# Sums of features and column products of a gated mixture of experts: which engine adds, which engine carries

## Chip, core and metric

One Trainium2 chip, one core. The metric is the device time of one launch in microseconds (us). Engine names in the profile: PE is TensorE's matmuls and PEld its weight loads, DVE is VectorE, ACT is ScalarE, POOL is GpSimd, SP is SyncE, which issues most transfers.

## What is computed

For each of 8 sequences (512 rows of 256 features, float32) eight experts and one shared expert are computed, weighted and added to the input:

```python
def _L0_cond_ref(hidden_states, gating_probs, shared_gate_prob, Wg, Wu, Wd, Sg, Su, Sd):
    E, B, S, D, F = (8, 2, 256, 256, 1024)
    h = hidden_states
    g = jnp.einsum('bsd,edf->ebsf', h, Wg)
    u = jnp.einsum('bsd,edf->ebsf', h, Wu)
    expert_outs = jnp.einsum('ebsf,efd->ebsd', jax.nn.silu(g) * u, Wd)
    expert_output = jnp.einsum('be,ebsd->bsd', gating_probs, expert_outs)
    shared = jnp.einsum('bsf,fd->bsd', jax.nn.silu(h @ Sg) * (h @ Su), Sd)
    sg = shared_gate_prob[:, :, None]
    return (1.0 - sg) * expert_output + sg * shared
x = x + _L0_cond_ref(x, ...)
```

The first line's sizes are not used; the arrays have 8 sequences of 512 rows, weights of 256 x 1024 and 1024 x 256 and nine experts with the shared one.

## The kernel before

**Units.** The work is cut into 36 units: two halves of four sequences, nine experts, two groups of four blocks of 128 hidden features. A unit takes four sequences times four blocks, 16 pairs (i, j), and finds the gate and the up product of each pair with fewer matmuls than the plain way: sums and differences of weight blocks and of sequences are made first, and results are shared between pair (i, j) and pair (j, i). `PAIRS` lists the six such couples. A unit whose `opens` is set is the first of a half, one whose `closes` is set the last.

**Two generators.** `gate_up` yields 52 steps per unit, one matmul each: 16 hub steps (`P_step`, `Q_step` for the four pairs (i, i), and the first couple's `R1_step`), then six per couple (`R1_step`, `R_step`). `finish` applies silu on ScalarE (L391) and makes the weighted feature block h on VectorE (L396). `down` yields 26 steps per unit, one matmul each, on two PSUM banks po0 and po1 that take turns: three for each couple (r, s or S, and a third with X, the difference of two h), four row products p0 to p3 and four column products q0 to q3, in the order 0, 1, 2, 3, 4, p0, q0, 5, q1, p1, q2, p2, q3, p3.

**Order.** The string `ORDER` interleaves them, two G (a step of `gate_up`) to one D (a step of `down`). `down` of a unit begins at its 22nd G, so the row and column products of a unit run in the hub of the next unit and just behind it. The order on PE and POOL is that of the program (`HAND`); after the first unit the order on ACT and DVE is chosen by the scheduler that places the instructions.

**Feature sums.** A row product needs the sum over j of h[i, j], a column product the sum over i of h[i, j]. `h_sums` puts four entries per couple into the list `u.sums`, 24 per unit; the entries of couple (i, j) are rows i, cols j, rows j, cols i. `add_sum` (L480) takes the first of the list and makes one GpSimd addition of 128 x 512 (L486). The first addition to a sum adds the diagonal block h[n, n] and another, with a new tile from `sumpool`. The main loop calls `add_sum` on every second G after the 22nd, and in the next unit on every G until the list is empty; `flush_sums` makes what is still missing before a product needs it.

**Accumulation.** Results of `down` gather over the units of a half in SBUF tiles `acc`: B for columns, b for rows, V and S for parts of both. `put` adds a bank into such a tile on VectorE (L516 to L520), or copies on ScalarE when the tile is new. `carried` does it through the bank: `seeded` takes the next bank with `new_po`, ScalarE copies the tile into it (L528), the matmul accumulates on top (L529), and ScalarE copies the bank back (L537). If the tile is new, or the bank was last used for a transpose (`turned`), the matmul starts from zero and `put` follows. The rows use `carried`; the columns use `single` (a matmul that starts from zero) and `put`. A closing unit also uses the bank of a column product, `done`, to form the final tiles.

**Work beside it.** From the third unit on, every fifth D takes a step of `prepare(1)`, which transposes the second half's input and forms its sums (POOL lines L211 to L217).

Of the kernel before, what the change touches and what calls it, by code (L numbers as in the profile page):

```python
# [11 lines left out]
ALU = mybir.AluOpType  # L12
# [4 lines left out]
def kernel(  # L17
# [38 lines left out]
    B, S, D = x.shape  # L56
# [38 lines left out]
    gp = nc.gpsimd  # L95
    ve = nc.vector
# [35 lines left out]
    def new_po(name, turns=False):  # L132

        k = po_next[0]
        if held[k]:
            k = 1 - k
        if not turns:
            po_next[0] = 1 - k
        return ps_o.tile([P, S], F32, tag=f"po{k}", name=name), k
# [144 lines left out]
    for h in range(NH):  # L284
        for e in range(NE):
            for g in range(GRP):
                u = Unit()
                u.n, u.h, u.e, u.g = len(units), h, e, g
                u.opens = e == 0 and g == 0
                u.closes = e == NE - 1 and g == GRP - 1  # L290
                u.name = f"{h}_{e}_{g}"
                u.raw, u.at, u.U, u.W, u.V, u.VB = {}, {}, {}, {}, {}, {}
                u.Ps, u.Ds, u.f, u.bank, u.h_ = {}, {}, {}, {}, {}
                u.sg, u.rows, u.cols, u.X, u.store = {}, {}, {}, {}, []
                u.sums = []
                u.ad, u.Ud, u.Wd = {}, {}, {}
                units.append(u)

# [181 lines left out]
    def add_sum(u):  # L480
        which, n, at = u.sums.pop(0)
        sums = getattr(u, which)
        first = n not in sums
        if first:
            sums[n] = sumpool.tile([P, S], F32, tag="sum", name=f"{which}{n}_{u.name}")
        gp.tensor_tensor(sums[n], u.h_[n, n] if first else sums[n], u.h_[at], ALU.add)  # L486

    def flush_sums(u, which, n):
        while any(w == which and k == n for w, k, _ in u.sums):
            add_sum(u)  # L490
# [5 lines left out]
    def closes(u, p):  # L496

        return u.closes and starred(u, p) or u.n + 2 == len(units) and p >= 4

    def down(u, acc):  # L500

        def tile_of(key):
            acc[key] = apool.tile(
                [P, S], F32, tag=f"acc{key[0]}{key[1]}", name=f"acc{key[0]}{key[1]}_{u.h}"
            )
            return acc[key]

        def put(key, bank, s):

            if key not in acc:  # L510
                if s == 1.0:
                    nc.scalar.copy(tile_of(key), bank)
                else:
                    nc.scalar.mul(tile_of(key), bank, s)
            elif s == 1.0:
                ve.tensor_add(acc[key], bank, acc[key])  # L516
            elif s == -1.0:
                ve.tensor_sub(acc[key], acc[key], bank)
            else:
                ve.scalar_tensor_tensor(acc[key], bank, s, acc[key], ALU.mult, ALU.add)  # L520

        def seeded(key, w, b):

            po, k = new_po(f"{key[0]}{key[1]}_{u.name}")
            full = key in acc and not turned[k]
            turned[k] = False
            if full:
                nc.scalar.copy(po, acc[key])  # L528
            nc.tensor.matmul(  # L529
                po, w, b, start=not full, stop=True, skip_group_check=full  # L530
            )
            return po, full

        def carried(key, w, b):
            po, full = seeded(key, w, b)
            if full:
                nc.scalar.copy(acc[key], po)  # L537
            else:
                put(key, po, 1.0)
            return po if full else acc[key]  # L540

        def single(key, w, b):
            po, k = new_po(f"{key[0]}{key[1]}_{u.name}")
            turned[k] = False
            nc.tensor.matmul(po, w, b, start=True, stop=True)  # L545
            return po, k

        def pair(p):
            i, j = PAIRS[p]
            d = CI[i] - CI[j]  # L550
            A, k = single(("r", p), u.Wd[p][i], u.h_[i, j])
            put(("B", j), A, 1.0)
            held[k] = True
            yield
            args = u.Wd[p][j], u.h_[j, i]
            if p in OWN and not closes(u, p):
                carried(("S", p), *args)
            else:
                if p in OWN:
                    o, full = seeded(("S", p), *args)  # L560
                    if not full:
                        ve.tensor_add(o, o, acc["S", p])
                else:
                    o, _ = single(("s", p), *args)
                put(("B", i), o, -1.0)
                put(("V", p), o, -1.0)
            yield
            nc.tensor.matmul(  # L568
                A, u.Ud[p], u.X[p], start=False, stop=True, skip_group_check=True
            )  # L570
            if closes(u, p):
                ve.tensor_add(A, A, acc["V", p])
                put(("b", i), A, 1.0 / d)
                put(("b", j), A, -1.0 / d)
            else:
                put(("V", p), A, 1.0)
            held[k] = False
            po_next[0] = 1 - k
            yield

        if u.n + 1 < len(units):
            order = (0, 1, 2, 3, 4, "p0", "q0", 5, "q1", "p1", "q2", "p2", "q3", "p3")
        else:
            order = (0, 1, 2, "q0", 3, "p0", "q3", "q1", "p3", "q2", "p1", "p2")
        done = {}
        for what in order:
            if isinstance(what, int):
                yield from pair(what)
                continue
            i = int(what[1])  # L590
            if what[0] == "p":
                flush_sums(u, "rows", i)
                done[what] = carried(("b", i), u.raw_d[:, i, 0:P], u.rows[i])
            else:
                flush_sums(u, "cols", i)
                po, _ = single(("q", i), u.ad[i], u.cols[i])
                put(("B", i), po, 1.0)
                done[what] = po
            if u.closes and f"p{i}" in done and f"q{i}" in done:
                if CI[i] != 0.0:  # L600
                    put(("B", i), done[f"p{i}"], -CI[i])
                for r in (0, 1):
                    ends[u.h, i, r] = acc["bB"[r], i]
            yield
# [183 lines left out]
    for u in units:  # L788
# [6 lines left out]
        for what in FIRST if u.n == 0 else LAST if nxt is None else ORDER:  # L795
            if what == "G":
                if nG == TAKE:
                    for _ in behind:
                        pass
                    if u.opens:  # L800
                        acc = {}
                    behind = down(u, acc)
# [7 lines left out]
                if nG > TAKE and nG % 2 == 0 or nxt is None:  # L810
                    for _ in range(2 if nxt is None else 1):
                        if u.sums:
                            add_sum(u)
                if nG < TAKE and u.n and units[u.n - 1].sums:
                    add_sum(units[u.n - 1])
# [7 lines left out]
            elif what == "X":  # L823
                i, j, pools = TAILS.pop(0)
# [59 lines left out]
```

## Time and profile before

Three runs gave 2463.46 us as a median (2463.18 to 2464.2).

| | us |
|---|---|
| profiled execution, its own time | 2464.21 |
| its span, first to last instruction | 2462.3 |
| PE busy in the span | 2439.2 |
| POOL busy | 2100.1 |
| DVE busy | 1936.5 |
| ACT busy | 1246.9 |
| mean granted TensorE clock | 0.999 of full speed |

The groups of instructions that the change touches, from the profile's table (line, engine, operation, output and inputs, shape, count; then busy us, mean ns of one, and idle time of the engine just before them):

```profile
L486 POOL TENSOR_TENSOR rows<-rows,h 128x512 f32<-128x512 f32 x284 | 373.9, 1316 | 0.0
L486 POOL TENSOR_TENSOR cols<-cols,h 128x512 f32<-128x512 f32 x284 | 363.3, 1279 | 0.0
L486 POOL TENSOR_TENSOR cols<-h,h 128x512 f32<-128x512 f32 x144 | 184.3, 1280 | 0.0
L516 DVE TENSOR_TENSOR accB<-q,accB 128x512 f32<-128x512 f32 x144 | 99.1, 688 | 41.7 <-PE q L545 41.3
L528 ACT COPY b<-accb 128x512 f32<-128x512 f32 x134 | 79.7, 595 | 52.6 <-DVE accV L518 39.2 <-DVE accB L516 5.1 <-DVE accb L520 3.4
L537 ACT COPY accb<-b 128x512 f32<-128x512 f32 x134 | 79.1, 590 | 36.5 <-PE b L529 33.7
L545 PE MATMUL q<-cols,ad 128*128 128x512 f32 x216 | 110.8, 595 | 4.8 <-POOL cols L486 3.3 <-DVE accB L520 1.4
```

One matmul of the program is two PE instructions in the trace, which overlap; a unit's length is read from the starts.

### The profile page before, as it was taken

The numbers are of one execution on the slowest core, as the hardware profiler recorded it, in microseconds if no ns is written. First come the engines' busy times: TensorE is split into PE (matmuls) and PEld (weight loads), VectorE is DVE, ScalarE is ACT, GpSimd is POOL, SyncE is SP. The second block draws the span as 40 slices with busy tenths as digits, with TensorE's granted clock in tenths as the row PEclk, the third lists the DMA queues.
The fourth block names the chain that finished last, engine by engine and source line by source line (L and its number), as shares of the span: only waits on it lengthen the run. The fifth ranks groups of instructions, "written<-read, shape, count | busy, mean of one in ns | idle before, by whom it ended". The sixth has DMA issues, their size and how long they took to land.

```text
span 2462.3 us, 22810 instructions
## 1 busy us (share of the span) xinstructions
PE 2439.2 (99%) x5772; PEld 1082.2 (44%) x5772; DVE 1936.5 (79%) x2880; ACT 1246.9 (51%) x2305; POOL 2100.1 (85%) x2339
## 2 busy tenths in 40 slices
PE   9999999999999999999999999999999999999998
PEld 3444444444444444444444444444444444444444
DVE  7777787787777777777987777777777777777788
ACT  4555445545555555445455555555555455555552
POOL 7988888898898998888878888888888888888884
PEclk9999999999999999999999999999999999999999
DMA  4333333443333333333443223323333333232332
GB/s 166 96 94 102 97 113 107 124 133 107 109 115 96 117 100 104 108 116 118 122 150 91 88 89 96 90 82 98 99 103 103 99 98 93 84 96 88 94 97 75
DMA packets 180800, 255.81 MB, mean 104 GB/s; under 512 B 14016, under 2 KB 114368, under 8 KB 180672
## 3 DMA queue, kind: packets, MB, share of 16 engines
q1 hardware_dynamic: 180384, 254.33, 33.9%
q8 instruction: 48, 0.79, 0.1%
q14 instruction: 80, 0.66, 0.1%
q10 hardware_dynamic: 288, 0.04, 0.0%
HBM read 238.59 MB, written 15.73 MB: 103 GB/s over the span
## 4 chain that ended last, share of the span: by engine, by line
PE 89%; POOL 6%; DVE 2%; issue 1%; DMA 1%; ACT 0%; SPq 0%; ACTq 0%; DVEq 0%; POOLq 0%
PE c L459 28%; PE c L449 14%; PE c L427 9%; PE c L405 8%; PE r L545 7%; PE r L568 7%; PE S L529 5%; PE b L529 5%; PE q L545 5%; PE s L545 2%; POOL cols L486 1%; POOL rows L486 1%; POOL wd L376 1%; DVE h L396 1%; POOL wb L343 0%
## 5 line engine op out<-in xcount | busy, mean ns | idle before, releaser
L459 PE MATMUL c<-b,wb 128*128 128x512 f32 x1728 | 847.2, 592 | 0.0
L391 ACT ACTIVATE sg<-c 128x512 f32<-128x512 f32 x576 | 343.9, 597 | 591.0 <-DVE c L464 336.1
L396 DVE SCALAR_TENSOR_TENSOR h<-sg,coef,c 128x512 f32<-128x512 f32 x576 | 428.1, 743 | 249.0 <-PE c L459 139.7
L459 PEld LDWEIGHTS c<-b,wb 128*128 128x128 f32 x1728 | 327.9, 190 | 411.0 <-issue 389.4
L449 PE MATMUL c<-v,u 128*128 128x512 f32 x864 | 441.7, 593 | 0.7 <-ACT c L444 0.7
L486 POOL TENSOR_TENSOR rows<-rows,h 128x512 f32<-128x512 f32 x284 | 373.9, 1316 | 0.0
L486 POOL TENSOR_TENSOR cols<-cols,h 128x512 f32<-128x512 f32 x284 | 363.3, 1279 | 0.0
L454 DVE TENSOR_TENSOR c<-D,c 128x512 f32<-128x512 f32 x432 | 299.0, 692 | 78.3 <-ACT sg L391 58.5
L464 DVE TENSOR_TENSOR c<-c,D 128x512 f32<-128x512 f32 x432 | 298.7, 691 | 20.2 <-PE c L459 20.0
L343 POOL TENSOR_TENSOR wb<-u,wb 128x256 f32<-128x256 f32 x108 | 78.8, 729 | 235.7 <-ACT wb L341 235.7
L405 PE MATMUL c<-x,w 128*128 128x512 f32 x576 | 278.1, 595 | 0.3 <-DVE x L166 0.3
L449 PEld LDWEIGHTS c<-v,u 128*128 128x128 f32 x864 | 162.9, 190 | 206.0 <-issue 165.6
L545 PE MATMUL r<-h,wd 128*128 128x512 f32 x428 | 218.8, 593 | 1.8 <-DVE accb L520 1.6
L568 PE MATMUL r<-X,ud 128*128 128x512 f32 x428 | 218.5, 592 | 0.0
L475 DVE TENSOR_TENSOR X<-h,h 128x512 f32<-128x512 f32 x214 | 211.6, 989 | 6.9
L427 PE MATMUL c<-x,at 128*128 128x512 f32 x432 | 209.6, 593 | 2.8 <-DVE P L420 2.7
L437 ACT COPY D<-c 128x512 f32<-128x512 f32 x284 | 166.0, 584 | 86.9 <-DVE h L396 86.9
L486 POOL TENSOR_TENSOR rows<-h,h 128x512 f32<-128x512 f32 x144 | 198.4, 1378 | 0.0
L486 POOL TENSOR_TENSOR cols<-h,h 128x512 f32<-128x512 f32 x144 | 184.3, 1280 | 0.0
L410 ACT COPY P<-c 128x512 f32<-128x512 f32 x216 | 126.7, 586 | 109.2 <-PE c L405 104.9
L405 PEld LDWEIGHTS c<-x,w 128*128 128x128 f32 x576 | 109.3, 191 | 135.1 <-issue 112.2
L528 ACT COPY S<-accS 128x512 f32<-128x512 f32 x135 | 79.7, 590 | 152.4 <-DVE accV L516 142.5
(106 smaller groups left out, 3480.8 us busy)
## 6 DMA issues: line engine op xcount, KB each, us to landing
b<-xs SPq DMA_DIRECT2D x210, 512.0 KB, 3.6
v<-xs SPq DMA_DIRECT2D x210, 256.0 KB, 2.6
w<-in_L_cond_Wg_dram SPq DMA_DIRECT2D x128, 128.0 KB, 3.5
w<-in_L_cond_Wu_dram SPq DMA_DIRECT2D x128, 128.0 KB, 3.6
wd<-in_L_cond_Wd_dram SPq DMA_DIRECT2D x32, 512.0 KB, 4.9
xin<-in_x_dram SPq DMA_DIRECT2D x24, 256.0 KB, 3.5
f<-xd SPq DMA_DIRECT2D x24, 256.0 KB, 3.2
xs<-f SPq DMA_DIRECT2D x18, 256.0 KB, 2.0
```

What stands on the lines that cost most here:

```text
L391: nc.scalar.activation(s, bank, AF.Silu)
L396: ve.scalar_tensor_tensor(t, u.sg[i, j], coef[:, u.e, b : b + 1], bank, ALU.mult, ALU.mult)
L405: nc.tensor.matmul(bank, u.raw[i][:, m, 0], xhub[u.h, i][:, 0], start=True, stop=True)
L427: nc.tensor.matmul(bank, u.at[i][:, m], xhub[u.h, i][:, 1], start=False, stop=True, skip_group_check=True,)
L449: nc.tensor.matmul(bank, u.U[p][:, m], u.V[p], start=False, stop=True, skip_group_check=True)
L454: ve.tensor_sub(other, u.Ds[j, m], bank)
L459: nc.tensor.matmul(bank, u.W[p][:, r, m], u.VB[p][:, r], start=False, stop=True, skip_group_check=True,)
L464: ve.tensor_add(bank, bank, u.Ds[j, m])
L486: gp.tensor_tensor(sums[n], u.h_[n, n] if first else sums[n], u.h_[at], ALU.add)
L529: nc.tensor.matmul(po, w, b, start=not full, stop=True, skip_group_check=full)
L545: nc.tensor.matmul(po, w, b, start=True, stop=True)
L568: nc.tensor.matmul(A, u.Ud[p], u.X[p], start=False, stop=True, skip_group_check=True)
```

## The change

Two edits. First, each unit counts its sums in `u.added`; the additions with number 3, 11 and 19 of the 24 (counted from 0) go to VectorE in units that neither open nor close a half. Second, the column products of all units but the two that close a half use `carried` with the key B, that is ScalarE's copy into the bank, an accumulating matmul and ScalarE's copy back, in place of a matmul from zero and VectorE's addition.

```diff
-                u.sums = []
+                u.sums, u.added = [], 0
...
-        gp.tensor_tensor(sums[n], u.h_[n, n] if first else sums[n], u.h_[at], ALU.add)
+        eng = ve if u.added % 8 == 3 and not (u.opens or u.closes) else gp
+        eng.tensor_tensor(sums[n], u.h_[n, n] if first else sums[n], u.h_[at], ALU.add)
+        u.added += 1
...
             else:
                 flush_sums(u, "cols", i)
+                if not u.closes:
+                    carried(("B", i), u.ad[i], u.cols[i])
+                    yield
+                    continue
                 po, _ = single(("q", i), u.ad[i], u.cols[i])
                 put(("B", i), po, 1.0)
                 done[what] = po
```

## The prediction

> **What bounds the kernel now.** I read four views, in this order: the busy shares, TensorE's own waits, TensorE's sequence unit by unit, and then the other engines beside it in one steady unit.
>
> ```profile
> span 2462.3 us, 22810 instructions
> PE 2439.2 (99%) x5772; PEld 1082.2 (44%) x5772; DVE 1936.5 (79%) x2880; ACT 1246.9 (51%) x2305; POOL 2100.1 (85%) x2339
> ```
>
> TensorE is busy for 99%, but a busy share does not say that matmuls run back to back, so the starts are needed. In the sequence of TensorE a single matmul is two instructions, and consecutive ones start 0.86 us apart (1453.07, 1453.93, 1454.79, ...). The same place in two neighbouring units, the two products (four instructions) that start at 1429.90 and at 1496.85, lies 66.95 us apart: 78 matmuls of 0.858 us, nothing over. Most of the 36 units are like this. TensorE is at its floor there, and no edit of other engines can shorten them; it can only lengthen them.
>
> What lies above the floor I got by taking, from each start to the next, the count of matmuls times 0.429 us per instruction (128-column transposes a quarter, 256-column products half). The work is 2423.4 us and the excess 33.5: 11.2 up to the end of the first unit, 8.6 in the last 95 us, and between them some 9 us of waits (the rest is missing records). What ended the waits between is in TensorE's list (total, times, longest):
>
> ```profile
> PE q L545 <- POOL cols L486: 3.3, 4, 1.2
> PE c L427 <- DVE P L420: 2.7, 3, 1.8
> PE S L529 <- ACT S L528: 1.7, 3, 0.6
> ```
>
> The first line is the one this change can touch: a column product waits for its sum on GpSimd. By start spacing those four cost 0.82 (at 96.43), 0.67 (638.98), 1.12 (841.06) and 1.35 us (1043.36). This is the costliest, first on TensorE and then on GpSimd:
>
> ```profile
> 1041.15 1.02 PE L427 MATMUL c<-x,at 128*128 128x512 f32 x2
> 1043.36 1.12 PE L545 MATMUL q<-cols,ad 128*128 128x512 f32 x2 [1.19 <-POOL cols L486]
> ...
> 1038.36 1.27 POOL L486 TENSOR_TENSOR cols<-cols,h 128x512 f32<-128x512 f32 x1
> 1039.58 1.28 POOL L486 TENSOR_TENSOR rows<-rows,h 128x512 f32<-128x512 f32 x1
> ...
> 1042.04 1.26 POOL L486 TENSOR_TENSOR cols<-cols,h 128x512 f32<-128x512 f32 x1
> ```
>
> The sum at 1042.04 feeds the product at 1043.36; GpSimd has no idle from 1008 to here, because this unit also carries steps of the second half's preparation (f, L211 to L217). The wait at 96.43 belongs to the sums of the first unit, which the change leaves on GpSimd.
>
> **The change part by part.** Own time of the profiled execution is 2464.21 us, 1.9 above its span and 0.75 above the median of 2463.46. The sum is made against 2464.21.
>
> (1) Three of 24 sums leave GpSimd in 32 units (36 less two that open and two that close a half): 96 x 1.28 us = 123 us off GpSimd. Counting calls, sums 3 and 11 fall in the unit itself (its 30th and 46th step), sum 19 in the next unit's hub (the 16 steps that mix x products of one's own block). In the view above sum 19 is the one at 1038.36, and the sum that q waits for is number 21 in the same queue. Without 19, number 21 starts 1.22 us earlier (1039.58 - 1038.36). Number 11 left the same unbroken queue 20 us before, worth up to another 1.2 us. That covers 0.67 and 1.12, and 1.35 with a little of number 11. Gain at most 0.67 + 1.12 + 1.35 = 3.1 us; at least 0, if GpSimd loses the time again. I take 2.8, nearest the upper end, since two of three are covered by sum 19 alone.
>
> (2) The three sums on VectorE. No such sum runs there now; the nearest is X, also two SBUF inputs and one SBUF output of the same size:
>
> ```profile
> L475 DVE TENSOR_TENSOR X<-h,h x214: 682/1056/1673, 38.1 to 2425.1; 128x512 f32<-128x512 f32 x107
> ```
>
> So 0.68 to 1.67, I take 1.06: 96 x 1.06 = 102 us more for VectorE. Where X runs beside GpSimd, one of the two is stretched: X is 0.69 at 1434.05, and the GpSimd addition that starts at 1434.11 takes 1.23 in place of 0.73; GpSimd's sums reach 1.73 in place of 1.27 (1493.81, with X at 1493.61). So a moved sum gives GpSimd 1.27 and takes up to 0.5 back. The Trainium skill, page "SBUF — State Buffer", section "Who interferes with whom", speaks against this edit: a VectorE instruction with two SBUF inputs holds a read port shared with GpSimd, and whichever starts second blocks until the other is done. The stretch of 0.5 agrees with it in kind; by the rule read strictly, a GpSimd sum would wait the whole 0.68 of an undisturbed sum, and the net gift would be 0.6 us a sum instead of 0.8.
>
> Cover for sums 3 and 11: VectorE waits 1.3 us in these blocks (before 1474.80 and 1490.25, both for a h buffer that GpSimd's rows still hold), and the next bank it must empty has slack: accV ends at 1477.47, the copy of S at 1478.1, its matmul starts 2.4 us later at 1480.54. Cover for sum 19: VectorE's idle 1.44 before 1436.84, and 0.57 plus the vanished addition of q0 (0.69) before 1439.44. Without cover a sum costs up to its 1.06 us of TensorE. I take 0.
>
> (3) The column product through its bank. There are four per unit in 34 units; rows already do this (134 copies in, 134 out), so about 134 again. VectorE loses 134 additions of 0.69 = 92 us; ScalarE gets 268 copies of 0.59 = 158 us. Over the span nothing is saturated: ScalarE goes from 1247 to 1405 us, VectorE from 1937 to 1946, GpSimd falls to 1977. But all column products fall into the hub and the block after it, so that stage decides:
>
> ```profile
> 1432.60:1453.20 20.60, 20.60 (x50) 9.12 (x49) 17.36 (x28) 11.99 (x22) 20.05 (x26) 1.00 0.11 31
> ```
>
> (TensorE, weight loads, VectorE, ScalarE, GpSimd, in 20.6 us.) ScalarE has 12.0 there and gets up to six copies, 3.5: 15.5 of 20.6, it fits. VectorE loses two additions (1.4) and gets sum 19 (0.7 to 1.2). A queue of its own does not run out; what can hurt is order. Each product's bank is needed two slots after it was used, 5.15 us. Before the product it must be emptied and filled:
>
> ```profile
> 1443.69 0.68 DVE L518 TENSOR_TENSOR accV<-accV,s 128x512 f32<-128x512 f32 x1
> 1444.79 0.75 DVE L396 SCALAR_TENSOR_TENSOR h<-sg,coef,c 128x512 f32<-128x512 f32 x1 [0.41 <-POOL rows L486]
> 1445.55 0.69 DVE L516 TENSOR_TENSOR accV<-r,accV 128x512 f32<-128x512 f32 x1
> 1446.41 3.68 DVE L420 TENSOR_TENSOR P<-P,c 128x512 f32<-128x512 f32 x6 [0.17 <-PE c L405]
> ...
> 1443.83 0.60 ACT L391 ACTIVATE sg<-c 128x512 f32<-128x512 f32 x1
> 1444.33 0.58 ACT L437 COPY D<-c 128x512 f32<-128x512 f32 x1
> 1445.57 0.59 ACT L437 COPY D<-c 128x512 f32<-128x512 f32 x1 [0.67 <-DVE h L396]
> 1446.27 0.59 ACT L528 COPY b<-accb 128x512 f32<-128x512 f32 x1
> ```
>
> q1 runs at 1447.06 in the bank that accV leaves at 1444.37. The new copy fits into ScalarE's idle 0.67 before 1445.57 and ends near 1445.5: slack 1.5 us. q0 (1436.76) follows accV at 1432.67 to 1433.36 with 2.8 us of slack for one copy. q1's copy out meets 2.98 idle before 1449.84; q2's out and q3's in meet 0.88 + 0.49 + 0.26 + 0.39 idle between 1452.4 and 1457.4, against 1.2. So I take 0 for TensorE. What is queued behind such a copy is the silu and D copies, and behind them h, the six f's at 1446.41 and the product at 1448.78: three f's, 0.60 apart, end at 1448.29, leaving 0.5 us. That is the thinnest cover in the unit. If a copy stands ahead of the silu at 1443.83, it ends at 1444.96, the silu at 1445.6, h starts 0.8 late, 0.17 of that is absorbed, and the f's are some 0.6 late: TensorE loses 0.1, and with the 0.16 that a restart adds (1.35 against 1.19 above) about 0.3. Bounds for (3): 0 to 0.3 a unit; were sum 19 also put just before the f's, 0.8 + 1.06 - 0.17 - 0.5 + 0.16 = 1.35, which I count with the second rival. A gain is excluded in steady units, which have no wait to give.
>
> **Sum.** 2464.21 - 2.8 + 0 + 0 = 2461.4 own time; 0.75 lower as a median, 2460.7 us.
>
> **The rivals.** About 0.2%, 4.9 us, is what can be told from no change.
>
> Hub late (slower): the copy into a column's bank stands in ScalarE's order ahead of the silu, as worked out. For it: ScalarE's and VectorE's order are not written by hand there, and the copies of S already stand waiting for accV, 142.5 us in 94 times, 1.5 each. Against: the same copies for rows cost TensorE nothing in steady units. 34 x 0.3 = 10.2: 2470.9; it decides from 0.5 us of lateness of the f's on. Chance 0.30.
>
> VectorE late (slower): a moved sum in the wrong place, as sum 3 or 11 before accV, delays S. In the closing unit three extra VectorE instructions (r and two on accb) do that, 0.72 us each time; one sum of 1.06 is less than their 1.9. If it happened once per unit, 32 x 0.72 = 23: 2484 (with 1.35 as above, 2504). Chance 0.08.
>
> No effect: GpSimd gains nothing where it matters, since sum 23 on GpSimd now waits for 19 on VectorE, or the stretch eats the gift: 2463.5. Chance 0.12.
>
> Faster beyond 0.2%: all 3.1 and both waits for accS ahead of transposes (1.12 and 0.97, at 194 and 339), 5.2: 2458.3. Nothing in the change leads to the second part. Chance 0.07.
>
> **How the numbers follow.** The forecast has 0.43, its own range 2459.5 to 2463. Of the hub rival's 0.30, 0.07 lies below 2468.4. Within 0.2%: 0.43 + 0.12 + 0.07 = 0.62; slower 0.23 + 0.08 = 0.31; faster 0.07. The range 2458.2 to 2473 leaves out that rival's 0.08, some 0.05 of the hub's end and 0.03 below.
>
> **What would show it.** Right: units still 66.95 us apart; no wait of a column product for GpSimd after the second unit; GpSimd near 1977 us, ScalarE near 1405. Hub late: waits of the matmuls behind L420, or of q for the copy in, in most units. VectorE late: waits of S for ScalarE in ordinary units. The prediction is wrong if units are longer than 67.1 us in steady stretches.

## The result, and the profile after

| | before | after |
|---|---|---|
| median, us (22 runs each, side by side) | 2463.21 | 2467.58 |
| profiled execution, its own time | 2464.21 | 2467.75 |
| its span | 2462.3 | 2465.8 |

The ratio is 1.0016, 95% interval 1.0010 to 1.0022: 4.4 us slower, where 2.8 us faster was forecast. (One run of each, 8235 us of after and 2857 of before, stands apart from all others and is used in no reading.) The time lies in the range of 2458.2 to 2473.0; its direction does not agree with the forecast. The busy shares of the kernel after:

```profile
PE 2443.7 (99%) x5772; PEld 1080.0 (44%) x5772; DVE 1967.8 (80%) x2842; ACT 1377.1 (56%) x2573; POOL 2020.1 (82%) x2243
```

Work moved as described: GpSimd has lost 96 instructions and 80 us, ScalarE has gained 268 copies. None of the engines beside TensorE has become full. The groups that the change made (busy us and mean ns of one, then idle time just before them):

```profile
L487 DVE TENSOR_TENSOR cols<-h,h 128x512 f32<-128x512 f32 x64 | 86.8, 1355 | 0.0
L530 ACT COPY B<-accB 128x512 f32<-128x512 f32 x134 | 80.4, 600 | 41.6 <-DVE accV L518 40.5
L539 ACT COPY accB<-B 128x512 f32<-128x512 f32 x134 | 78.4, 585 | 41.1 <-PE B L531 41.1
L487 DVE TENSOR_TENSOR cols<-cols,h 128x512 f32<-128x512 f32 x32 | 39.8, 1242 | 0.0
```

A sum on VectorE takes 1.24 to 1.36 us on average, not the 1.06 assumed. TensorE's own waits in the kernel after (total us, times, longest):

```profile
PE ptx L143 <- ACT accS L539: 2.9, 2, 1.9
...
PE B L531 <- POOL cols L487: 0.6, 1, 0.6
```

Against the list of before: column products wait for GpSimd once instead of four times (the one left stands at 95 us, in the opening unit's sums), so the three waits of 3.1 us in all are gone. The transposes of the second half's input wait longer (2.9 instead of 1.8). Nothing in the list is as large as the loss, because the largest part of it is too short for this list. It shows in the starts: the unit that the prediction measured, from 1429.90 to 1496.85, is now the pair at 1430.99 and 1498.07, 67.08 us apart instead of 66.95. The 0.13 more stand at one place in each unit. TensorE's sequence there:

```profile
1476.48 1.02 PE L570 MATMUL r<-X,ud 128*128 128x512 f32 x2
1477.39 1.10 PE L449 MATMUL c<-v,u 128*128 128x512 f32 x2
1478.33 1.02 PE L459 MATMUL c<-b,wb 128*128 128x512 f32 x2
```

The matmul at 1477.39 was due at 1476.48 + 0.86 = 1477.34, 0.05 late; the next one follows after 0.94 instead of 0.86, 0.08 more. So 0.13 a unit, and 32 x 0.13 = 4.2 us. What it waits for is on VectorE and ScalarE (the number in brackets is idle time before the instruction and what ended it):

```profile
1470.76 0.74 DVE L396 SCALAR_TENSOR_TENSOR h<-sg,coef,c 128x512 f32<-128x512 f32 x1
1471.41 1.35 DVE L487 TENSOR_TENSOR cols<-h,h 128x512 f32<-128x512 f32 x1
1472.68 1.21 DVE L475 TENSOR_TENSOR X<-h,h 128x512 f32<-128x512 f32 x1
1473.81 0.68 DVE L454 TENSOR_TENSOR c<-D,c 128x512 f32<-128x512 f32 x1
1474.41 0.68 DVE L518 TENSOR_TENSOR accB<-r,accB 128x512 f32<-128x512 f32 x1
1475.01 0.68 DVE L464 TENSOR_TENSOR c<-c,D 128x512 f32<-128x512 f32 x1
...
1475.73 0.60 ACT L391 ACTIVATE sg<-c 128x512 f32<-128x512 f32 x1 [3.11 <-DVE c L464]
1476.22 0.58 ACT L539 COPY accS<-S 128x512 f32<-128x512 f32 x1
1476.69 0.61 ACT L444 COPY c<-P 128x512 f32<-128x512 f32 x1
```

The same instructions of before:

```profile
1470.43 1.23 DVE L475 TENSOR_TENSOR X<-h,h 128x512 f32<-128x512 f32 x1
...
1472.79 0.68 DVE L464 TENSOR_TENSOR c<-c,D 128x512 f32<-128x512 f32 x1
...
1473.50 0.60 ACT L391 ACTIVATE sg<-c 128x512 f32<-128x512 f32 x1 [1.98 <-DVE c L464]
1474.13 0.59 ACT L444 COPY c<-P 128x512 f32<-128x512 f32 x1
1474.66 0.58 ACT L537 COPY accS<-S 128x512 f32<-128x512 f32 x1
...
1476.25 1.02 PE L449 MATMUL c<-v,u 128*128 128x512 f32 x2
```

The reader is to see a chain that crosses three engines: sum 3 stands ahead of X on VectorE, so X, L454, accB and L464 come later; ScalarE's silu waits for L464 (3.11 instead of 1.98); behind the silu stand the copy of S and the copy that seeds the next couple's bank (L444), and TensorE's L449 accumulates onto that bank. Measured against TensorE, the seed ended at 1474.72, 1.53 before its matmul; now it ends at 1477.30, 0.04 before the matmul was due. The matmul starts 0.09 after that end by these rows, hence 0.05 late; in all 31 units where the trace has both records, the distance is 0.10 by the unrounded times. The 1.49 lost are the sum, 1.27 from its start to X's, less about 0.14, and about 0.35 for the copy of S, which ScalarE now makes between the silu and the seed.

The sum of the traces' differences: 4.2 (32 units), 0.5 (a wait of 0.47 at 2377 us in the last unit for a carried column's copy in), -3.1 (the column products' waits), 1.1 (the wait at 339 us), 1.7 (TensorE's clock just behind it), 0.6 (once at 531 us), -1.1 (the start) = 3.9. The spans differ by 3.5; some matmul records are missing, which the difference of 0.4 may be.

### The profile page after: what moved, and what is told of

Same layout as the page of the kernel before. It is cut to its first block, busy times and chain, and to the rows that moved or that the text cites. A ratio compares the mean times of both kernels' runs of the same rounds, so it can differ in the third digit from the quotient of the medians.

```text
span 2465.8 us, 23011 instructions
## 1 busy us (share of the span) xinstructions
PE 2443.7 (99%) x5772; PEld 1080.0 (44%) x5772; DVE 1967.8 (80%) x2842; ACT 1377.1 (56%) x2573; POOL 2020.1 (82%) x2243
## 4 chain that ended last, share of the span: by engine, by line
PE 94%; DVE 3%; POOL 1%; issue 1%; ACT 0%; DMA 0%; SPq 0%; DVEq 0%; ACTq 0%; POOLq 0%
PE c L459 29%; PE c L449 14%; PE c L427 9%; PE c L405 9%; PE r L547 7%; PE r L570 7%; PE S L531 5%; PE b L531 5%; PE B L531 5%; PE s L547 2%; DVE h L396 1%; POOL cols L487 0%; PE tail L657 0%; POOL rows L487 0%; DVE X L475 0%
## 5 line engine op out<-in xcount | busy, mean ns | idle before, releaser
L459 PE MATMUL c<-b,wb 128*128 128x512 f32 x1728 | 848.3, 593 | 0.0
L459 PEld LDWEIGHTS c<-b,wb 128*128 128x128 f32 x1728 | 328.1, 190 | 411.1 <-issue 392.5
L449 PE MATMUL c<-v,u 128*128 128x512 f32 x864 | 444.1, 595 | 2.0 <-ACT c L444 1.5
L454 DVE TENSOR_TENSOR c<-D,c 128x512 f32<-128x512 f32 x432 | 299.2, 693 | 136.6 <-ACT sg L391 94.0
L487 POOL TENSOR_TENSOR cols<-cols,h 128x512 f32<-128x512 f32 x252 | 335.8, 1333 | 0.0
L343 POOL TENSOR_TENSOR wb<-u,wb 128x256 f32<-128x256 f32 x108 | 78.7, 729 | 278.9 <-ACT wb L341 278.9
L464 DVE TENSOR_TENSOR c<-c,D 128x512 f32<-128x512 f32 x432 | 298.2, 690 | 5.5 <-PE c L459 2.9
L449 PEld LDWEIGHTS c<-v,u 128*128 128x128 f32 x864 | 160.3, 189 | 214.2 <-issue 163.6
L475 DVE TENSOR_TENSOR X<-h,h 128x512 f32<-128x512 f32 x214 | 222.3, 1039 | 4.7
L570 PE MATMUL r<-X,ud 128*128 128x512 f32 x428 | 219.1, 594 | 0.0
L343 POOL TENSOR_TENSOR wb<-u,w 128x256 f32<-128x256 f32 x108 | 89.0, 824 | 94.9 <-PE c L459 91.7
L531 PE MATMUL S<-h,wd 128*128 128x512 f32 x288 | 147.9, 595 | 1.8 <-ACT S L530 1.7
```

What stands on the lines that cost most here:

```text
L449: nc.tensor.matmul(bank, u.U[p][:, m], u.V[p], start=False, stop=True, skip_group_check=True)
L454: ve.tensor_sub(other, u.Ds[j, m], bank)
L459: nc.tensor.matmul(bank, u.W[p][:, r, m], u.VB[p][:, r], start=False, stop=True, skip_group_check=True,)
L464: ve.tensor_add(bank, bank, u.Ds[j, m])
L487: eng.tensor_tensor(sums[n], u.h_[n, n] if first else sums[n], u.h_[at], ALU.add)
L531: nc.tensor.matmul(po, w, b, start=not full, stop=True, skip_group_check=full)
```

## The experiments

All edits are made to the changed kernel. Where only the condition of the moved sums differs, the diff gives that line. Each was timed beside the kernel before, whose median was between 2463.0 and 2463.2 us in all of them. The theory: a sum that stands ahead of L464 on VectorE uses up the 1.53 us that the seed copy had. The rival: the carried columns' copies, on ScalarE, make something late.

**The two halves of the change.** Columns carried alone (cols_only):

```diff
-        eng = ve if u.added % 8 == 3 and not (u.opens or u.closes) else gp
+        eng = ve if False else gp
```

> The column products are carried through their bank, no sum is moved. Theory (a sum on VectorE in the third block of a unit delays the seed copy ahead of a matmul of L449 by 0.13 us in each of 32 units): units are 66.95 us apart again, the three waits of column products for GpSimd (0.7 to 1.4 us each) are back, 2463 to 2464 us. Rival (ScalarE's copies of the columns in the hub cost the time): units stay at 67.08 us, 2467 us or more.

Sums moved alone (sums_only):

```diff
-                if not u.closes:
-                    carried(("B", i), u.ad[i], u.cols[i])
-                    yield
-                    continue
```

> Sums 3, 11 and 19 on VectorE, the column products as in the kernel before. Theory: units 67.08 us apart or longer with the small waits at L449 in the third block, no wait of a column product for GpSimd after the second unit, 2466 to 2468 us. Rival (the columns' copies): units 66.95 us apart, 2460 to 2461 us.

Measured: cols_only 2464.2 us, ratio 1.0005 (0.9995 to 1.0014); sums_only 2466.87, ratio 1.0015 (1.0006 to 1.0024). In cols_only units are 66.95 us apart and the three waits for GpSimd are back. TensorE's waits there:

```profile
PE B L531 <- POOL cols L487: 3.4, 4, 1.2
```

This is the old line of q under a new name: same four times, same longest. In sums_only the units have the 0.13, and none of these three waits is there. So the lengthening of the units belongs to the sums, and the rival falls: the carrying of columns leaves the units as they were and is close to neutral in the median.

**Which of the three sums.** cols_s19, cols_s11_19 and cols_s3 carry the columns and move only these sums:

```diff
+        eng = ve if u.added == 19 and not (u.opens or u.closes) else gp
...
+        eng = ve if u.added in (11, 19) and not (u.opens or u.closes) else gp
...
+        eng = ve if u.added == 3 and not (u.opens or u.closes) else gp
```

> Columns carried, of the three sums only number 19 on VectorE. Theory: units 66.95 us apart, the waits of column products for GpSimd in the units at 639, 841 and 1043 us gone or under 0.3 us each, no drop of the granted clock at 339 us: 2460 to 2461 us. Rival (columns' copies): 2467 us. Rival (GpSimd needs all three to be relieved): the three waits stay, 2463 us.

> Columns carried, sums 11 and 19 on VectorE, 3 back on GpSimd. Theory: units 66.95 us apart; the transposes at 339 us still wait about 2 us, since sum 11 stands in the block before them, and the clock drops behind them in some runs: 2461 to 2463 us. If sum 11 is as harmful per unit as sum 3, units are 67.08 us apart and the time is 2466 us.

> Columns carried, of the three sums only number 3 on VectorE. Theory (sum 3 alone is the cost): units 67.08 us apart, with the small wait at L449 in the third block of each; the three waits of column products for GpSimd partly back; 2466 to 2468 us. If the loss needs sums 3 and 11 together, units are 66.95 us apart and the time is 2463 us.

| | median us | ratio (95%) | unit | waits of column products for GpSimd behind the start |
|---|---|---|---|---|
| cols_s19 | 2461.47 | 0.9993 (0.9984 to 1.0003) | 66.95 | none at 639, 0.34, 0.60 |
| cols_s11_19 | 2461.41 | 0.9994 (0.9985 to 1.0004) | 66.95 | none |
| cols_s3 | 2468.78 | 1.0026 (1.0015 to 1.0036) | 67.08 | 0.68, 1.13, 1.37 |

One sum out of three carries the whole lengthening of the units. The time of cols_s3 is 0.8 above the range expected: besides 32 times 0.13 its trace has 0.59 at 528 us, in place of one of the 0.05, and the 0.47 in the last unit, 5.2 in all against 5.6 by the medians. cols_s19 keeps more of the waits than expected (under 0.3 each) and is 0.5 above its range. Sums 11 and 19 together give what the prediction said of all three: no waits and unlengthened units. Sum 3 gives all the harm and none of the relief, which had been expected in part. The relief is lost at a line that stands between it and the column products. GpSimd at 1007 us in cols_s3 (in the kernel before, the same instruction stands at 1006.78 with 2.04 of idle time ahead of it):

```profile
1007.80 0.73 POOL L343 TENSOR_TENSOR wb<-u,wb 128x256 f32<-128x256 f32 x1 [2.18 <-ACT wb L341]
```

GpSimd idles here for ScalarE's wb whether sum 3 was its own or not. The time of sum 3 was gone even before this: GpSimd's addition beside it, at 995.95, takes 1.72 instead of 1.26, and ahead of L343 at 999.36 GpSimd idles for 1.70 instead of 0.92, where it waits for TensorE. Time given to GpSimd ahead of an idle stretch only lengthens the idle stretch; sums 11 and 19 are behind it, in the stretch without idle that ends in the wait.

**More of the suspected cost.** cols_s3x2 is cols_s3 (with its condition) and makes sum 3's addition twice, with the same result:

```diff
-        eng.tensor_tensor(sums[n], u.h_[n, n] if first else sums[n], u.h_[at], ALU.add)
+        for _ in range(2 if eng is ve else 1):
+            eng.tensor_tensor(sums[n], u.h_[n, n] if first else sums[n], u.h_[at], ALU.add)
```

> As cols_s3, but VectorE makes addition number 3 twice (the second writes the same sum again), so the suspected delay is doubled. Theory: the first addition uses up the slack before the seed copy of L444, so the second lands on TensorE nearly whole, 0.7 to 1.4 us more per unit, 32 times: units 67.8 to 68.4 us apart, 2488 to 2511 us. If the 0.13 us is a fixed price of a handover between engines and not lateness, units stay at 67.1 to 67.2 us and the time is under 2471 us.

Measured: 2480.15 us, ratio 1.0069 (1.0054 to 1.0084). The direction is as expected, the size is not: most units are 67.33 to 67.35 apart, against 67.08 in cols_s3, where 67.8 to 68.4 was expected. VectorE, ScalarE and TensorE in cols_s3x2:

```profile
1483.38 0.68 DVE L488 TENSOR_TENSOR cols<-h,h 128x512 f32<-128x512 f32 x1
...
1483.38 0.59 ACT L540 COPY accS<-S 128x512 f32<-128x512 f32 x1 [2.40 <-PE S L532]
1484.70 0.60 ACT L391 ACTIVATE sg<-c 128x512 f32<-128x512 f32 x1 [0.73 <-DVE c L464]
1485.33 0.59 ACT L444 COPY c<-P 128x512 f32<-128x512 f32 x1
...
1486.02 1.10 PE L449 MATMUL c<-v,u 128*128 128x512 f32 x2 [0.16 <-POOL wb L343]
```

The second addition ran where GpSimd did not disturb it, 0.60 from its start to that of L464 (1483.98), and the copy of S now stands ahead of the silu, which gives the 0.35 back. 0.61 - 0.35 = 0.26, and the wait before L449 rose from 0.05 to 0.31. (The bracket names GpSimd's L343, which ended at 1485.82; the seed ended later, at 1485.92, and the matmul started 0.10 after it, as it started 0.09 after its seed in the kernel after.) Three units are different: at 188, 532 and 736 us the second addition overlaps with one of GpSimd and takes 1.25 to 1.78 instead of 0.68, and L449 is 1.29, 1.43 and 1.41 late, the size expected of all; there too it starts 0.10 after the end of its seed. So once the slack is gone, lateness of the seed passes to TensorE one to one, in small and in large. This is what makes the cause a measured one, and not only a coincidence in time.

**The same work at another place.** If it is the place and not VectorE's load, another sum must be free. cols_s7 moves number 7 alone:

```diff
+        eng = ve if u.added == 7 and not (u.opens or u.closes) else gp
```

> Columns carried, of 24 sums only number 7 on VectorE: the same work per unit as cols_s3, but VectorE makes it behind the addition of L464 that the silu and the seed copy wait for, and not ahead of it. Theory (place, not load, is the cost): units 66.95 us apart, 2462 to 2464 us. If the load of one more addition per unit or the port shared with GpSimd is the cost: units 67.05 us or more, 2466 us or more.

Measured: 2463.65 us, ratio 1.0001 (0.9992 to 1.0011), units 66.95 apart. VectorE in cols_s7:

```profile
1471.65 0.68 DVE L464 TENSOR_TENSOR c<-c,D 128x512 f32<-128x512 f32 x1
1472.25 0.68 DVE L487 TENSOR_TENSOR cols<-cols,h 128x512 f32<-128x512 f32 x1
1473.60 0.75 DVE L396 SCALAR_TENSOR_TENSOR h<-sg,coef,c 128x512 f32<-128x512 f32 x1 [0.67 <-PE c L459]
```

The sum stands behind L464, in idle time of which 0.67 are still left, and costs nothing, although it makes GpSimd's addition at 1472.31 take 1.75. It also gains nothing: the three waits for GpSimd are still there (0.66, 1.09, 1.38), as it too is ahead of the idle stretch.

cols_s8 moves number 8 alone:

```diff
+        eng = ve if u.added == 8 and not (u.opens or u.closes) else gp
```

> Columns carried, of 24 sums only number 8 on VectorE: it stands ahead of X and of the addition of L464 as sum 3 does, but one block later, where VectorE waited 1.8 us for TensorE before (1482.53 us in the trace of before). Theory (a block with slack takes the sum): units 66.95 us apart, 2463 to 2464.5 us. If every place ahead of X costs: 67.05 us or more, 2466 us or more.

Measured: 2460.94 us, ratio 0.9990 (0.9981 to 1.0000), with units 66.95 apart and none of the three waits; the range expected, 2463 to 2464.5, had not counted on these. VectorE, ScalarE and TensorE in cols_s8:

```profile
1473.96 0.79 DVE L487 TENSOR_TENSOR rows<-h,h 128x512 f32<-128x512 f32 x1
1474.68 1.21 DVE L475 TENSOR_TENSOR X<-h,h 128x512 f32<-128x512 f32 x1
...
1477.01 0.68 DVE L464 TENSOR_TENSOR c<-c,D 128x512 f32<-128x512 f32 x1
...
1478.68 0.61 ACT L444 COPY c<-P 128x512 f32<-128x512 f32 x1
...
1479.89 1.02 PE L449 MATMUL c<-v,u 128*128 128x512 f32 x2
```

It stands ahead of X as sum 3 does, in the next block. It takes 0.72 from its start to X's, where sum 3 takes 1.27, since only the last 0.25 of a GpSimd sum (1472.93 to 1474.21) overlaps with it; but X behind it takes 1.21 instead of 0.69, and measured against TensorE L464 comes 1.09 later. With the copy of S ahead of the seed, 1.43 are lost, nearly as many as the 1.49 of sum 3. What differs is the slack. The seed and its matmul in this block of before:

```profile
1481.35 0.59 ACT L444 COPY c<-P 128x512 f32<-128x512 f32 x1
...
1483.97 1.02 PE L449 MATMUL c<-v,u 128*128 128x512 f32 x2
```

The seed ended at 1481.94, 2.03 before its matmul, not 1.53. cols_s8 therefore says what a block with more slack takes, and nothing of the third block. Now the seed ends at 1479.29, 0.60 before its matmul: the slack is used, not used up. And number 8 leaves GpSimd's queue behind the idle stretch, so this one sum takes away all three waits.

**The wait at 339 us.** In the kernel after, the profile has a second loss: ahead of four transposes of the second half's input, in the unit with number 4 (counted from 0). ScalarE and TensorE there:

```profile
337.95 0.60 ACT L391 ACTIVATE sg<-c 128x512 f32<-128x512 f32 x1 [3.12 <-DVE c L464]
338.44 0.58 ACT L539 COPY accS<-S 128x512 f32<-128x512 f32 x1
...
339.07 0.66 PE L143 MATMUL ptx<-ident,xin 128*128 128x128 f32 x4 [1.94 <-ACT accS L539]
339.57 3.02 PE L459 MATMUL c<-b,wb 128*128 128x512 f32 x4
342.39 1.62 PE L570 MATMUL r<-X,ud 128*128 128x512 f32 x2
```

This is sum 11, on VectorE from 333.62 to 334.98: again the silu is late, and the copy of S, which frees the bank for the transposes, stands behind it. Four matmuls of L459 then take 2.82 to the next start instead of 1.72, and the two of L570 take 1.45 (to 343.84) instead of 0.86: 1.7 us more. The windows of after say why (busy us of TensorE, weight loads, VectorE, ScalarE, GpSimd, granted clock, share of transfers and GB/s):

```profile
336.00:339.00 3.00, 1.14 (x3) 0.19 (x1) 1.91 (x4) 1.05 (x2) 3.00 (x3) 1.00 0.34 93
339.00:341.00 2.00, 1.93 (x7) 1.20 (x8) 0.01 (x1) 0.61 (x2) 2.00 (x3) 0.79 0.00 0
341.00:343.00 2.00, 2.00 (x3) 0.68 (x3) 1.81 (x3) 0.00 (x0) 1.92 (x3) 0.50 0.34 131
343.00:345.00 2.00, 2.00 (x5) 0.90 (x4) 1.28 (x3) 0.10 (x1) 2.00 (x3) 0.85 0.60 182
```

The clock granted fell to 0.50 behind the wait, for about 3.4 us: what the last three rows lack of 1.00 is 0.42, 1.00 and 0.30 us of full clock, 1.7 us in all, the same as the loss. The same window of sums_only, which has the same wait (1.93):

```profile
341.00:343.00 2.00, 2.00 (x6) 0.95 (x5) 1.97 (x4) 0.07 (x1) 1.92 (x3) 1.00 0.70 218
```

There the clock stayed at 1.00. To see what the wait is worth, after_but11 leaves this one sum, in this one unit, on GpSimd:

```diff
-        eng = ve if u.added % 8 == 3 and not (u.opens or u.closes) else gp
+        eng = ve if u.added % 8 == 3 and not (u.opens or u.closes) and (u.n, u.added) != (4, 11) else gp
```

> The changed kernel, but sum 11 of the fifth unit (n = 4) alone goes back to GpSimd. Theory (that one sum makes the transposes at 339 us wait 2 us in place of 1, and in part of the runs the TensorE clock is halved behind so long a wait): the wait is back at 1.0 us, no granted clock under 1.00 at 339 to 344 us in the profile, the runs lie within 1 us of each other and the time is 2465.5 to 2466.3 us (2467.6 with the sum there). If the spread of the changed kernel has another cause, runs still spread over 2 us or more.

Measured: 2465.42 us, ratio 1.0009 (0.9999 to 1.0018), just below what was expected; the wait is back at 0.97 by start spacing, where after has 2.09. One addition of 1.36 us, out of 96, costs about 2467.58 - 2465.42 = 2.2 us of the median. The ten runs also lie within 1.0 us of each other (2464.69 to 2465.65), where those of after reach from 2465.95 to 2468.84.

**A version without the harm.** s19_s11late leaves sum 3 on GpSimd everywhere and sum 11 too in the first units, moves sum 19 in the opening units as well, and does not carry the columns; best_cols is the same with columns carried:

```diff
-        eng = ve if u.added % 8 == 3 and not (u.opens or u.closes) else gp
+        eng = ve if (u.added == 19 or u.added == 11 and u.n > 6) and not u.closes else gp
...
-                if not u.closes:
-                    carried(("B", i), u.ad[i], u.cols[i])
-                    yield
-                    continue
```

> Column products as in the kernel before; sum 19 on VectorE in all units but the two that close a half, sum 11 only from the eighth unit on, sum 3 on GpSimd. Theory: units 66.95 us apart, no wait of a column product for GpSimd at 639, 841 and 1043 us, the one at 95 us shorter (0.8 us before), the transposes at 339 us wait 1 us as before and the clock stays: 2458.5 to 2460.5 us, the fastest of all. If carried columns were part of the gain of cols_s19, it is slower than 2461.4 us.

> As s19_s11late, with the column products carried through their bank as well: what carrying is worth by itself where no sum is in the way. Theory (carrying neither helps nor harms in a steady unit): units 66.95 us apart, one new wait of 0.5 us in the last unit for the copy in, 2459.5 to 2460.3 us. If carrying relieves VectorE where it counts: under 2459 us. If the copies cost: 2462 us or more.

Measured: s19_s11late 2459.5 us, ratio 0.9985 (0.9976 to 0.9994), the fastest of all and faster than both kernels; best_cols 2460.02, ratio 0.9987 (0.9978 to 0.9996). In TensorE's waits in s19_s11late no line of a column product waiting for GpSimd is left, that of the opening unit included. Carrying the columns makes no difference that can be told here; its profile has one wait more, 0.47 at 2369 us in the last unit.

## Why the prediction was wrong

**(1) Sums off GpSimd, "I take 2.8": right.** All three waits are gone (3.1 us), the fourth stayed, as stated. The net gift of 0.8 us a sum fits: with sum 19 alone the waits of 1.12 and 1.35 became 0.34 and 0.60. What the step did not see is that the three sums are worth different amounts: 19 and 11 give it, 3 gives nothing.

**(2) "Cover for sums 3 and 11 ... I take 0": this step failed.** It named as cover VectorE's 1.3 us of idle before 1474.80, and as the next deadline the copy of S with 2.4 us of slack. Both were read correctly and neither decides. The idle stands behind L464, and the sum was put ahead of it; cols_s7, whose sum does stand behind L464, shows that this cover is real. The deadline that ends first is on another engine: L464, silu, seed copy, with 1.53 us, shorter than the 2.4 that were measured. It was in the trace of before; the prediction followed the sum only to the next bank that VectorE must empty. 0.13 us a unit, 4.2 in all, came of it, and from sum 11 in one unit 1.1 more, with 1.7 of slowed clock behind it.

A term beside it was sized too low: 1.06 us for a sum, where the runs have 1.24 to 1.36 when a GpSimd addition is under way and 0.68 when the sum starts first (cols_s7). By an estimate it mattered: of 1.53 the copy of S takes 0.35 and the way from the seed to the matmul 0.09, and 0.14 is won back, which leaves 1.23. A sum of 1.06 would just have passed; one of 1.27 does not. No run has a sum of 1.06 at this place. The Trainium skill, page "SBUF — State Buffer", section "Who interferes with whom", says that the instruction that starts second waits until the other gives the shared read port back. Here it agrees with the row: GpSimd's rows sum started at 1470.94 for 1.27, the VectorE sum at 1471.41 ended 0.55 after it, not quite the 0.68 of an undisturbed sum. The prediction used that rule for what GpSimd gets back and not for the sum itself.

**(3) Columns carried, "I take 0": right in the steady units.** They are 66.95 us apart in cols_only. The rival "hub late", at 0.30, needed a copy ahead of the silu in the hub, and no such loss shows; one wait of 0.47 in the last unit was not foreseen.

**The rivals.** "VectorE late", at 0.08, named the engine and sum 3 and expected 0.72 us a unit by way of accV and S, 23 us in all. The cause was of that kind; the way was by the seed, and the price was only what exceeded the slack. That the time still lies inside the stated range is luck: the range reached that far up for the hub rival, whose mechanism did not occur. The criterion for a wrong prediction, units longer than 67.1 us, was set a little too wide to catch it: they are 67.08. "No effect" does not hold for the three sums, but describes sum 3 alone on GpSimd's side.

**What no step had.** The wait at 339 us and the clock behind it: the prediction named this wait (0.97) as something that might shrink, and not as one that a late silu lengthens. In the fifth block of a unit sum 11 makes the silu as late as sum 3 does, and costs nothing, since no seed copy follows there; in the unit with number 4 a transpose wants the bank instead.

**What stays open.** Why the clock fell in the profile of after and not in two others with the same wait. The spans of after's runs are 2463.8 to 2464.4 in six cases and 2464.8 to 2466.2 in the 15 others. The profile with the clock at 0.50 is of the second group (2465.8); the one of sums_only with 1.00 is of that kernel's shorter group (2463.1, where eight of its ten runs have 2464.5 to 2465.9). Each run's mean clock, on record to three places, fits: it is 0.999 in all eight longer runs of sums_only and 1.000 in the two shorter, 0.999 in the two longest of cols_s11_19 and 1.000 in its eight others, and 0.999 in all 15 longer runs of after, but also in three of its six shorter ones. Four runs of after_but11 have 0.999 without being longer than the rest. So that the clock divides the groups is likely; where it fell in each run was not recorded.

## What to carry to other kernels

When work is put onto an engine that does not bound the kernel, follow every instruction behind it on that engine, across the other engines, to the bounding one, and compare the shortest slack with the new work's duration: idle time behind the critical instruction is no cover for work placed ahead of it. In these runs time taken off a queue helped only in the stretch without idle that ends in the wait; ahead of an idle stretch it was lost there. Moving one or two well-placed items can be worth more than moving all that fit into the busy totals.

## What the runs showed of the hardware

A TensorE wait of 1.94 us was followed in one profile by a granted clock of 0.50 for about 3.4 us, which added 1.7 us, and in two others (sums_only, cols_s11_19) by no change at all. The Trainium skill, page "TensorE: Matmul & The Clock Gate", section "What's actually happening", gives at least one idle window of about 3.4 us as the condition for the slow clock, and says that this window runs freely and does not start with the kernel. The length of the slow stretch agrees with such a window, and the change from run to run would fit a free-running one. The condition does not fit as stated, as 1.94 us of matmul idle sufficed here, and the measurement decides.

A short wait of TensorE costs more than itself: 0.05 us of lateness at 1477.39 was followed by 0.08 more before the next matmul, so most of the 4.2 us is not waiting but starting again. The addition hardly grows with the wait: it is again 0.07 to 0.08 behind the 0.31 and the 1.4 of cols_s3x2, and 0.10 behind the 1.35 of before. The prediction's 0.16 for a restart, 1.35 less 1.19, set the spacing of starts against an idle time between modelled ends and starts, and is not this quantity.
